# Two batches of an attention layer handled as one unit, with PSUM divided three to five

## Chip, cores, metric

One core of a Trainium2 chip. Times are device microseconds of one execution; the runs of one kernel agree within 0.1% here.

## The reference, cut

Input x is [128 batches, 128 nodes, 512 features], fp32.

```python
# layer 0: h = relu(layernorm(x)); a max over an expression of adj @ h; collapses to one number per node
h = jnp.maximum(_layernorm(x, axis=-1), 0.0)
x = x + _L0_gnn_ref(h, adj, adj, L0_gnn_b)
# layer 1: attention with 8 heads of 64, masked by adj
h = jnp.maximum(_layernorm(x, axis=-1), 0.0)
x = x + _L1_gnn_ref(h, adj, Wq, bq, Wk, bk, Wv, bv)
#   q, k, v = h @ W + b;  scores = q k^T / 8;  masked softmax over j;  out = weights @ v
```

What layer 0 adds is one number per node and batch, and the second layernorm does not see it. So the kernel normalises once, gets layer 0 from one "adjacency" matmul per batch (adj times h, then a maximum), and runs projections, scores and the product with v. A further column of ones in v makes the softmax sums. The projections of four batches are done together, each of q, k and v with seven block products instead of eight (p1 to p7 below; each is a "projection group" of 8 matmuls in the trace). The seven products need sums of blocks of h, which VectorE makes: the "h sums" below.

## The kernel before

```python
        ps_mm = ctx.enter_context(tc.tile_pool(name="ps_mm", bufs=4, space=PSUM))
        ps_sc = ctx.enter_context(tc.tile_pool(name="ps_sc", bufs=1, space=PSUM))
        ps_av = ctx.enter_context(tc.tile_pool(name="ps_av", bufs=1, space=PSUM))
        # ... (cut: loads, constants)
            # norm(m), statistics
            st = stat.tile([P, 6], F32, name="st")
            mv = stat.tile([P, 2], F32, name="mv")
            nc.vector.bn_stats(st, X[g][:, i, :])
            nc.vector.bn_aggr(mv, st)
            ve = stat.tile([P, 1], F32, name="ve")
            nc.vector.tensor_scalar_add(ve, mv[:, 1:2], EPS)
            rstd = RSTD[m] = stat.tile([P, 1], F32, name="rstd")
            nc.gpsimd.tensor_tensor(rstd, ve, mhalf, op=ALU.pow)
            MV[m] = mv

        def norm_end(m):
            g, i = divmod(m, G)
            nc.vector.tensor_scalar(
                HN[m], X[g][:, i, :], MV[m][:, 0:1], 0.0, op0=ALU.subtract, op1=ALU.max
            )
            nc.scalar.activation(HN[m], HN[m], AF.Copy, scale=RSTD[m])
            if m >= G:
                add_bv(m)
        # ... (cut: blocks, move, transposes)
        def adjacency(m):
            g, i = divmod(m, G)
            if m >= 2 * G + 2:
                pa = ps_mm.tile([P, 512], F32, name="mm")
            else:
                if i % 2 == 0:
                    PA[g] = ps_av.tile([P, 2, 512], F32, name="pav")
                pa = PA[g][:, i % 2]
            nc.tensor.matmul(pa, adjT, HN[m], start=True, stop=True)
            nc.vector.reduce_max(AMAX[g][:, i : i + 1], pa, axis=AX.X)
            if i == G - 1:
                nc.vector.tensor_scalar(C[g], AMAX[g], b0_sb, 0.0, op0=ALU.add, op1=ALU.max)
        # ... (cut: the sums of the seven-product scheme, class Products)
            q, k, v = PR[g + 1] = [Products(g + 1, n) for n in "qkv"]
            return (
                (q.p1, last, q.p6, q.p2, q.p7),
                (q.p5, q.p4, k.p1, k.p6, q.p3),
                (k.p2, k.p7, k.p5, k.p4, v.p1),
                (k.p3, v.p6, v.p2, v.p7, v.p5, v.p4),
            )
        # ... (cut)
        def scores(g, i, spare=False):

            psc = ps_sc.tile([P, 2, NC, D], F32, name="sc")
            for f in range(NC):
                for j in range(2):
                    r = slice(j * HD, (j + 1) * HD)
                    nc.tensor.matmul(
                        psc[:, j, f, :],
                        KT[g][r, f, i * D : (i + 1) * D],
                        QT[g][r, f, i * D : (i + 1) * D],
                        start=True, stop=True,
                    )
            if spare:
                w = spare_tile().rearrange("p (j f d) -> p j f d", j=2, f=NC)
            else:
                w = work.tile([P, 2, NC, D], F32, name="w")
            for j in range(2):
                nc.scalar.activation(w[:, j], psc[:, j], AF.Exp, scale=HD ** -0.5)
            return w
        # ... (cut: masks: w *= live, two calls on VectorE)
        def finish(g, i, w, spare=False, eng=nc.vector):
            b = g * G + i
            if spare:
                pav = ps_sc.tile([P, 2, NC, D], F32, name="sc").rearrange("p j f d -> p j (f d)")
            else:
                pav = ps_av.tile([P, 2, 512], F32, name="pav")

            for h in range(H):
                for k in range(2):
                    r = slice(k * HD, (k + 1) * HD)
                    nc.tensor.matmul(
                        pav[r, h // 4, (h % 4) * HE : (h % 4 + 1) * HE],
                        w[:, h % 2, h // 2, r], V[g % 2][:, i, h, :],
                        start=True, stop=True,
                    )
            po = pav[:, :, 0 : 4 * HE].rearrange("p k (h e) -> p k h e", e=HE)
            rs = RS[:, b].rearrange("p (k h) -> p k h", k=2)
            nc.vector.reciprocal(rs, po[:, :, :, HD])
            if b < B - 2:
                o = work.tile([P, 2, 4, HD], F32, name="o")
            else:
                o = tmp.tile([P, 2, HT2], F32, name="p1b").rearrange("p k (h d) -> p k h d", d=HD)
            nc.vector.tensor_tensor(
                o, po[:, :, :, 0:HD], rs.unsqueeze(3).to_broadcast([P, 2, 4, HD]), op=ALU.mult
            )
            y = o.rearrange("p k h d -> p (k h d)")
            x_b, c_b = X[g][:, i, :], C[g][:, i : i + 1]
            if eng is nc.vector:
                eng.scalar_tensor_tensor(y, x_b, c_b, y, op0=ALU.add, op1=ALU.add)
            else:
                nc.scalar.activation(x_b, x_b, AF.Identity, bias=c_b)
                eng.tensor_tensor(y, x_b, y, op=ALU.add)
            nc.sync.dma_start(out[b], y)
        # ... (cut: count, prologue)
            for b in range(B - G - 1):
                g, i = divmod(b, G)
                m = b + 2 * G + 2
                if i == 0 and g + 3 < NG:
                    load(g + 3)
                if i == 0:
                    parts = products(g)
                w = scores(g, i)
                if g == 0:
                    add_bv(b)
                for s in range(max(5, len(parts[i]))):
                    if s < len(parts[i]):
                        parts[i][s]()
                    if s == 0:
                        masks(w)
                    elif s == 3 and b == B - 2 * G + 1:
                        count(0, B - 2 * G)
                    elif i == G - 1 and g + 2 < NG and s < 5:
                        h_sum(g + 2, s - 1)
                    if m < B:
                        if s == 1:
                            norm(m)
                        elif s == 2:
                            norm_end(m)
                        elif s == 4:
                            blocks(m)
                if m < B:
                    adjacency(m)
                finish(g, i, w)
                if m < B:
                    move(m)
            # ... (cut: the last five batches by hand)
```

Of the kernel before, what the change touches and what calls it, by code (L numbers as in the profile page):

```python
# [161 lines left out]
def tile_adj_preln_d2(  # L163
# [36 lines left out]
    def fast(ctx):  # L200
# [5 lines left out]
        ps_mm = ctx.enter_context(tc.tile_pool(name="ps_mm", bufs=4, space=PSUM))  # L206
        ps_sc = ctx.enter_context(tc.tile_pool(name="ps_sc", bufs=1, space=PSUM))
        ps_av = ctx.enter_context(tc.tile_pool(name="ps_av", bufs=1, space=PSUM))

        CNT = []  # L210
        X, HN, TB, HT, HB, QT, KT, C, AMAX, WA, RSTD, MV, PR, PH, PA = ({} for _ in range(15))
# [94 lines left out]
        def transposes(m):  # L306
            g, i = divmod(m, G)
            if i % 2 == 0:
                PH[g] = ps_sc.tile([P, 2, NC, D], F32, name="sc")
            ph = PH[g][:, i % 2]  # L310
            for c in range(NC):
                nc.tensor.transpose(ph[:, c], HN[m][:, c * P : (c + 1) * P], ident)  # L312
            nc.scalar.copy(HT[g][:, i], ph)

        def adjacency(m):
            g, i = divmod(m, G)
            if m >= 2 * G + 2:
                pa = ps_mm.tile([P, 512], F32, name="mm")
            else:
                if i % 2 == 0:  # L320
                    PA[g] = ps_av.tile([P, 2, 512], F32, name="pav")
                pa = PA[g][:, i % 2]
# [149 lines left out]
        def products(g):  # L472


            if g not in PR:
                PR[g] = [Products(g, n) for n in "qkv"]
            last = PR[g][2].p3
            if g + 1 == NG:
                return (last,), (), (), ()
            q, k, v = PR[g + 1] = [Products(g + 1, n) for n in "qkv"]  # L480
            return (
                (q.p1, last, q.p6, q.p2, q.p7),
                (q.p5, q.p4, k.p1, k.p6, q.p3),
                (k.p2, k.p7, k.p5, k.p4, v.p1),
                (k.p3, v.p6, v.p2, v.p7, v.p5, v.p4),
            )
# [6 lines left out]
        def scores(g, i, spare=False):  # L493

            psc = ps_sc.tile([P, 2, NC, D], F32, name="sc")
            for f in range(NC):
                for j in range(2):
                    r = slice(j * HD, (j + 1) * HD)
                    nc.tensor.matmul(  # L499
                        psc[:, j, f, :],  # L500
# [8 lines left out]
            for j in range(2):  # L509
                nc.scalar.activation(w[:, j], psc[:, j], AF.Exp, scale=HD ** -0.5)  # L510
            return w

        def masks(w):
# [3 lines left out]
        def finish(g, i, w, spare=False, eng=nc.vector):  # L517
            b = g * G + i
            if spare:
                pav = ps_sc.tile([P, 2, NC, D], F32, name="sc").rearrange("p j f d -> p j (f d)")  # L520
            else:
                pav = ps_av.tile([P, 2, 512], F32, name="pav")

            for h in range(H):
                for k in range(2):
                    r = slice(k * HD, (k + 1) * HD)
                    nc.tensor.matmul(  # L527
                        pav[r, h // 4, (h % 4) * HE : (h % 4 + 1) * HE],
                        w[:, h % 2, h // 2, r], V[g % 2][:, i, h, :],
                        start=True, stop=True,  # L530
                    )
            po = pav[:, :, 0 : 4 * HE].rearrange("p k (h e) -> p k h e", e=HE)
            rs = RS[:, b].rearrange("p (k h) -> p k h", k=2)
            nc.vector.reciprocal(rs, po[:, :, :, HD])
            if b < B - 2:
                o = work.tile([P, 2, 4, HD], F32, name="o")
            else:
                o = tmp.tile([P, 2, HT2], F32, name="p1b").rearrange("p k (h d) -> p k h d", d=HD)
            nc.vector.tensor_tensor(
                o, po[:, :, :, 0:HD], rs.unsqueeze(3).to_broadcast([P, 2, 4, HD]), op=ALU.mult  # L540
            )
            y = o.rearrange("p k h d -> p (k h d)")
# [19 lines left out]
        with tc.manual_schedule():  # L562
# [43 lines left out]
            move(2 * G + 1)  # L606
            for b in range(B - G - 1):
                g, i = divmod(b, G)
                m = b + 2 * G + 2
                if i == 0 and g + 3 < NG:  # L610
                    load(g + 3)
                if i == 0:
                    parts = products(g)
                w = scores(g, i)
                if g == 0:
                    add_bv(b)
                for s in range(max(5, len(parts[i]))):
                    if s < len(parts[i]):
                        parts[i][s]()
                    if s == 0:  # L620
                        masks(w)
                    elif s == 3 and b == B - 2 * G + 1:
                        count(0, B - 2 * G)
                    elif i == G - 1 and g + 2 < NG and s < 5:
                        h_sum(g + 2, s - 1)
                    if m < B:
                        if s == 1:
                            norm(m)
                        elif s == 2:
                            norm_end(m)  # L630
                        elif s == 4:
                            blocks(m)
                if m < B:
                    adjacency(m)
                finish(g, i, w)
                if m < B:
                    move(m)
# [69 lines left out]
```

## Time and profile before

| | before |
|---|---|
| time, median of 3 runs | 1602.29 us (1601.85 to 1602.46) |
| span of the profiled run | 1599.8 us |
| TensorE busy | 1584.6 us |
| VectorE busy | 1112.2 us (70%) |
| order on TensorE, per batch | adjacency, products with v, scores, 5 or 6 projection groups |

How to read it: what TensorE gets done is read from the starts of its matmuls. A row of the timeline is a run of like instructions: start, length from first start to last end, engine, line, out<-in, the part of the array used (rows*columns), shape, count. The length includes a tail that overlaps the next row (one projection matmul's row is 0.38 us long, the next starts after 0.216); the difference of two starts does not.

### The profile page before, as it was taken

To read this page: it belongs to the slowest core of one execution; us is meant where nothing else is said; L and a number is where in the kernel's file an instruction comes from. 1 tells how busy PE (TensorE), PEld (TensorE's weight loads), DVE (VectorE), ACT (ScalarE), POOL (GpSimd) and SP (SyncE) were. 2 spreads that over 40 slices of the span, in tenths; PEclk is the share of its full clock that TensorE was granted. 3 is DMA by queue.
4 is the path that set the end of the run, shared out by engine and by line. 5 is a ranking of instruction groups with operands and counts; after the bars stand their busy time and mean duration, and the time that the engine had idled before them with its cause. 6 is when DMAs were issued, how large, how long until landed. Compare 5 with 4: busy or idle time off the path is not lost.

```text
span 1599.8 us, 29471 instructions
## 1 busy us (share of the span) xinstructions
PE 1584.6 (99%) x11821; PEld 1319.4 (82%) x11821; DVE 1112.2 (70%) x2044; ACT 424.5 (27%) x848; POOL 264.0 (17%) x281
## 2 busy tenths in 40 slices
PE   7999999999999999999999999999999999999998
PEld 5788888888888888888888888888888888888886
DVE  4777677776777776776767677677777677676655
ACT  3222222222222222222222222222222222222222
POOL 4421111111111111111111111111111111111101
PEclk9999999999999999999999999999999999999999
DMA  4022322123222232222232212322223322223111
GB/s 166 16 69 69 80 64 69 41 70 77 68 65 46 69 73 72 69 48 64 68 80 65 68 42 72 73 68 66 46 69 72 73 69 53 58 68 80 40 28 48
DMA packets 299082, 104.02 MB, mean 65 GB/s; under 512 B 264448, under 2 KB 264576, under 8 KB 298944
## 3 DMA queue, kind: packets, MB, share of 16 engines
q1 hardware_dynamic: 297520, 99.69, 24.8%
q8 instruction: 94, 1.54, 0.4%
q10 hardware_dynamic: 1248, 2.16, 0.4%
q14 instruction: 44, 0.36, 0.1%
q0 software_dynamic: 176, 0.27, 0.1%
HBM read 37.03 MB, written 33.55 MB: 44 GB/s over the span
## 4 chain that ended last, share of the span: by engine, by line
PE 99%; DVE 1%; DMA 0%; ACT 0%; POOL 0%; issue 0%; POOLq 0%; ACTq 0%
PE mm L389 73%; PE sc L499 9%; PE pav L527 8%; PE mm L323 6%; PE mm L460 1%; PE pav L323 1%; PE sc L312 0%; DMA xg<-in_x_dram 0%; DVE tb L515 0%; DVE st L265 0%; DVE amax L324 0%; ACT hn L278 0%; POOL p1b L548 0%; PE sc L527 0%; DVE hn L275 0%
## 5 line engine op out<-in xcount | busy, mean ns | idle before, releaser
L270 POOL TENSOR_TENSOR rstd<-ve,mhalf 128x1 f32<-128x1 f32 x128 | 84.0, 656 | 1210.6 <-DVE ve L268 983.5
L510 ACT ACTIVATE w<-sc 128x512 f32<-128x512 f32 x252 | 136.8, 594 | 505.3 <-PE sc L499 505.3
L527 PEld LDWEIGHTS pav<-v,w 128*64 128x64 f32 x4032 | 127.8, 137 | 91.9 <-issue 47.8
L389 PE MATMUL mm<-hs,sq_sb 128*128 128x256 f32 x744 | 179.0, 383 | 0.0
L389 PE MATMUL mm<-sv_sb,hs 128*128 128x256 f32 x768 | 176.7, 379 | 0.0
L389 PE MATMUL mm<-hs,sk_sb 128*128 128x256 f32 x768 | 176.2, 379 | 0.0
L284 POOL TENSOR_TENSOR xg<-xg,bv_sb 128x512 f32<-128x512 f32 x128 | 163.3, 1277 | 30.2 <-DVE hn L275 28.4
L515 DVE TENSOR_TENSOR w<-w,live 128x512 f32<-128x512 f32 x252 | 162.1, 685 | 2.0 <-ACT w L510 2.0
L389 PEld LDWEIGHTS mm<-hs,sk_sb 128*128 128x128 f32 x768 | 145.9, 190 | 20.7 <-issue 1.0
L389 PEld LDWEIGHTS mm<-sv_sb,hs 128*128 128x128 f32 x768 | 145.8, 190 | 20.4 <-issue 0.5
L278 ACT ACTIVATE hn<-hn,rstd 128x512 f32<-128x512 f32 x126 | 91.4, 725 | 259.7 <-DVE hn L275 207.3
L389 PEld LDWEIGHTS mm<-hs,sq_sb 128*128 128x128 f32 x744 | 138.8, 190 | 21.4
L499 PE MATMUL sc<-qT,kT 64*128 64x128 f32 x2048 | 148.7, 285 | 0.0
L527 PE MATMUL pav<-v,w 128*64 128x65 f32 x4032 | 145.3, 224 | 0.0
L499 PEld LDWEIGHTS sc<-qT,kT 64*128 64x128 f32 x2048 | 124.2, 187 | 10.1 <-issue 1.7
L437 DVE TENSOR_TENSOR u<-mm,p1b 128x512 f32<-128x512 f32 x63 | 43.6, 691 | 126.4 <-PE mm L389 126.4
L389 PE MATMUL mm<-hT,wk_sb 128*128 128x256 f32 x512 | 124.2, 385 | 0.0
L389 PE MATMUL mm<-wv_sb,hT 128*128 128x256 f32 x512 | 121.0, 379 | 0.0
L323 PE MATMUL mm<-hn,adjT 128*128 128x512 f32 x236 | 120.5, 592 | 0.0
L389 PE MATMUL mm<-hT,wq_sb 128*128 128x256 f32 x496 | 120.4, 386 | 0.0
L389 PEld LDWEIGHTS mm<-wv_sb,hT 128*128 128x128 f32 x512 | 97.2, 190 | 13.7 <-issue 0.5
L389 PEld LDWEIGHTS mm<-hT,wk_sb 128*128 128x128 f32 x512 | 94.7, 190 | 15.4
(107 smaller groups left out, 2048.7 us busy)
## 6 DMA issues: line engine op xcount, KB each, us to landing
out_dram<-o SPq DMA_DIRECT2D x126, 256.0 KB, 2.1
xg<-in_x_dram SPq DMA_DIRECT2D x62, 512.0 KB, 5.2
hT<-tb SPq DMA_DIRECT2D x960, 32.0 KB, 1.9
xg<-in_x_dram SPq DMA_DIRECT2D x2, 256.0 KB, 3.3
xg<-in_x_dram ACTq DMA_DIRECT2D x2, 256.0 KB, 6.2
wq_sb<-in_L_gnn_Wq_dram SPq DMA_DIRECT2D x1, 512.0 KB, 8.7
wk_sb<-in_L_gnn_Wk_dram SPq DMA_DIRECT2D x1, 512.0 KB, 11.5
wq_sb<-in_L_gnn_Wq_dram ACTq DMA_DIRECT2D x1, 512.0 KB, 11.4
```

The lines of the kernel that those rows point to most:

```text
L270: nc.gpsimd.tensor_tensor(rstd, ve, mhalf, op=ALU.pow)
L278: nc.scalar.activation(HN[m], HN[m], AF.Copy, scale=RSTD[m])
L284: nc.gpsimd.tensor_tensor(x_m, x_m, bv_sb, op=ALU.add)
L323: nc.tensor.matmul(pa, adjT, HN[m], start=True, stop=True)
L389: nc.tensor.matmul(bank[:, r, :], lhs, rhs, start=first and r == 0 and c == 0, stop=r == 1 and c == 1, skip_group_check=True,)
L437: nc.vector.tensor_tensor(self.u3, self.b, self.pf[1], op=ALU.add)
L460: nc.tensor.matmul(bank[:, r, :], W["q"][:, c, (2 * f + r) * P : (2 * f + r + 1) * P], h[:, :, c], start=r == 0 and c == 0, stop=r == 1 an ...
L499: nc.tensor.matmul(psc[:, j, f, :], KT[g][r, f, i * D : (i + 1) * D], QT[g][r, f, i * D : (i + 1) * D], start=True, stop=True,)
L510: nc.scalar.activation(w[:, j], psc[:, j], AF.Exp, scale=HD ** -0.5)
L515: nc.vector.tensor_tensor(w[:, j], w[:, j], live_h, op=ALU.mult)
L527: nc.tensor.matmul(pav[r, h // 4, (h % 4) * HE : (h % 4 + 1) * HE], w[:, h % 2, h // 2, r], V[g % 2][:, i, h, :], start=True, stop=True,)
```

## The change

Its intent: let TensorE change between its three forms of use (128*128, 128*64, 64*128) once for two batches instead of once for each. For this, products and scores of two batches have to stand side by side, so PSUM, where TensorE's results go, is divided anew. It holds eight banks of 128 x 512 fp32 values in this kernel: before, four for projections, two for scores and two for products; now, three banks for projections, five that the products (banks 0, 1, 2), the scores (3 and 4 for the even batch, 0 and 2 for the odd one), the adjacency products (0, 1) and the first transposes share. Heads 0 to 6 of a batch fill one bank, head 7 of both goes into bank 1. The loop is rewritten in units of two batches.

```diff
-        ps_mm = ctx.enter_context(tc.tile_pool(name="ps_mm", bufs=4, space=PSUM))
-        ps_sc = ctx.enter_context(tc.tile_pool(name="ps_sc", bufs=1, space=PSUM))
-        ps_av = ctx.enter_context(tc.tile_pool(name="ps_av", bufs=1, space=PSUM))
+        ps_mm = ctx.enter_context(tc.tile_pool(name="ps_mm", bufs=3, space=PSUM))
+        ps_at = ctx.enter_context(tc.tile_pool(name="ps_at", bufs=1, space=PSUM))
...  (adjacency: pa = bank(i % 2); scores: banks (3, 4) or (0, 2))
-                (q.p1, last, q.p6, q.p2, q.p7),
-                (q.p5, q.p4, k.p1, k.p6, q.p3),
-                (k.p2, k.p7, k.p5, k.p4, v.p1),
-                (k.p3, v.p6, v.p2, v.p7, v.p5, v.p4),
+                (q.p1, last, q.p6, q.p2, q.p7, q.p5, q.p4, k.p1, q.p3, k.p6),
+                (k.p2, k.p7, k.p5, k.p4, v.p1, k.p3, v.p6, v.p2, v.p7, v.p5, v.p4),
...  (finish is split: apply(b) has the products of two batches and their evictions, residual(b) the rest)
+        def apply(b):
+            one = bank(0), bank(1), bank(2)
+            for e in range(2):
+                g, i = divmod(b + e, G)
+                w = w_of.pop(b + e)
+                for h in range(H):
+                    pav, c = (one[2 * e], h * HE) if h < H - 1 else (one[1], e * HE)
...  (two matmuls each; then reciprocal and multiplication for bank 0, bank 2, bank 1)
+            for b in range(0, B - 3 * G // 2, 2):
...
+                if b > 0:
+                    apply(b - 2)
+                scores(b)
+                scores(b + 1)
+                for s, p in enumerate(part):
+                    if s < 2:
+                        if b > 0:
+                            residual(b - 2 + s)
+                        masks(b + s)
+                    p()
...
+                    if m < B:
+                        if s in (2, 4):
+                            norm(m + s // 2 - 1)
+                        elif s in (3, 5):
+                            norm_end(m + s // 2 - 1)
+                        elif s in (6, 7):
+                            blocks(m + s - 6)
+                        if s in (4, 7):
+                            adjacency(m + s // 7)
+                    if i == 2 and g + 2 < NG and 7 <= s < 11:
+                        h_sum(g + 2, s - 7)
...  (the last six batches are rewritten by hand)
```

More of the change, by code (lines that the diff above doesn't have):

```diff
@@ L205, in fast, with bank @@
         stat = ctx.enter_context(tc.tile_pool(name="stat", bufs=6))
-        ps_mm = ctx.enter_context(tc.tile_pool(name="ps_mm", bufs=4, space=PSUM))
-        ps_sc = ctx.enter_context(tc.tile_pool(name="ps_sc", bufs=1, space=PSUM))
-        ps_av = ctx.enter_context(tc.tile_pool(name="ps_av", bufs=1, space=PSUM))
-        CNT = []
-        X, HN, TB, HT, HB, QT, KT, C, AMAX, WA, RSTD, MV, PR, PH, PA = ({} for _ in range(15))
+        ps_mm = ctx.enter_context(tc.tile_pool(name="ps_mm", bufs=3, space=PSUM))
+        ps_at = ctx.enter_context(tc.tile_pool(name="ps_at", bufs=1, space=PSUM))
+        CNT, w_of, O = [], {}, {}
+        X, HN, TB, HT, HB, QT, KT, C, AMAX, WA, RSTD, MV, PR = ({} for _ in range(13))
+        def bank(k):
+            return ps_at.tile([P, 512], F32, name=f"at{k}")
         def load(g):
@@ L307, in transposes @@
             g, i = divmod(m, G)
-            if i % 2 == 0:
-                PH[g] = ps_sc.tile([P, 2, NC, D], F32, name="sc")
-            ph = PH[g][:, i % 2]
+            ph = bank(3 + i % 2).rearrange("p (c d) -> p c d", c=NC)
             for c in range(NC):
@@ L316, in adjacency @@
             g, i = divmod(m, G)
-            if m >= 2 * G + 2:
-                pa = ps_mm.tile([P, 512], F32, name="mm")
-            else:
-                if i % 2 == 0:
-                    PA[g] = ps_av.tile([P, 2, 512], F32, name="pav")
-                pa = PA[g][:, i % 2]
+            pa = bank(i % 2)
             nc.tensor.matmul(pa, adjT, HN[m], start=True, stop=True)
@@ L472, in products @@
         def products(g):
-            if g not in PR:
-                PR[g] = [Products(g, n) for n in "qkv"]
             last = PR[g][2].p3
             if g + 1 == NG:
-                return (last,), (), (), ()
+                return (last,), ()
             q, k, v = PR[g + 1] = [Products(g + 1, n) for n in "qkv"]
             return (
-                (q.p1, last, q.p6, q.p2, q.p7),
-                (q.p5, q.p4, k.p1, k.p6, q.p3),
-                (k.p2, k.p7, k.p5, k.p4, v.p1),
-                (k.p3, v.p6, v.p2, v.p7, v.p5, v.p4),
+                (q.p1, last, q.p6, q.p2, q.p7, q.p5, q.p4, k.p1, q.p3, k.p6),
+                (k.p2, k.p7, k.p5, k.p4, v.p1, k.p3, v.p6, v.p2, v.p7, v.p5, v.p4),
             )
@@ L491, in spare_tile, with scores @@
             return t.rearrange("p a i c r -> p (a i c r)")
-        def scores(g, i, spare=False):
-            psc = ps_sc.tile([P, 2, NC, D], F32, name="sc")
+        def scores(b, spare=False):
+            g, i = divmod(b, G)
+            psc = [
+                bank(k).rearrange("p (f d) -> p f d", f=NC) for k in ((3, 4), (0, 2))[b % 2]
+            ]
             for f in range(NC):
@@ L499, in scores @@
                     nc.tensor.matmul(
-                        psc[:, j, f, :],
+                        psc[j][:, f, :],
                         KT[g][r, f, i * D : (i + 1) * D],
@@ L509, in scores, with masks @@
             for j in range(2):
-                nc.scalar.activation(w[:, j], psc[:, j], AF.Exp, scale=HD ** -0.5)
-            return w
-        def masks(w):
+                nc.scalar.activation(w[:, j], psc[j], AF.Exp, scale=HD ** -0.5)
+            w_of[b] = w
+        def masks(b):
+            w = w_of[b]
             for j in range(2):
                 nc.vector.tensor_tensor(w[:, j], w[:, j], live_h, op=ALU.mult)
-        def finish(g, i, w, spare=False, eng=nc.vector):
-            b = g * G + i
-            if spare:
-                pav = ps_sc.tile([P, 2, NC, D], F32, name="sc").rearrange("p j f d -> p j (f d)")
-            else:
-                pav = ps_av.tile([P, 2, 512], F32, name="pav")
-            for h in range(H):
-                for k in range(2):
-                    r = slice(k * HD, (k + 1) * HD)
-                    nc.tensor.matmul(
-                        pav[r, h // 4, (h % 4) * HE : (h % 4 + 1) * HE],
-                        w[:, h % 2, h // 2, r], V[g % 2][:, i, h, :],
-                        start=True, stop=True,
-                    )
-            po = pav[:, :, 0 : 4 * HE].rearrange("p k (h e) -> p k h e", e=HE)
-            rs = RS[:, b].rearrange("p (k h) -> p k h", k=2)
-            nc.vector.reciprocal(rs, po[:, :, :, HD])
-            if b < B - 2:
-                o = work.tile([P, 2, 4, HD], F32, name="o")
-            else:
-                o = tmp.tile([P, 2, HT2], F32, name="p1b").rearrange("p k (h d) -> p k h d", d=HD)
-            nc.vector.tensor_tensor(
-                o, po[:, :, :, 0:HD], rs.unsqueeze(3).to_broadcast([P, 2, 4, HD]), op=ALU.mult
-            )
-            y = o.rearrange("p k h d -> p (k h d)")
@@ new lines, in apply @@
+        def apply(b):
[5 more added lines that the diff above has]
+                    pav, c = (one[2 * e], h * HE) if h < H - 1 else (one[1], e * HE)
+                    for k in range(2):
+                        r = slice(k * HD, (k + 1) * HD)
+                        nc.tensor.matmul(
+                            pav[r, c : c + HE], w[:, h % 2, h // 2, r], V[g % 2][:, i, h, :],
+                            start=True, stop=True,
+                        )
+            if b < B - 2:
+                o = work.tile([P, 2, N], F32, name="o", bufs=1)
+            else:
+                o = proj.tile([P, 4, 2, 2, D], F32, name="hs").rearrange(
+                    "p k i c d -> p k (i c d)"
+                )[:, 0:2]
+            O[b] = o
+            for e, h, n in ((0, 0, 7), (1, 0, 7), (None, 7, 1)):
+                if e is None:
+                    po = one[1][:, 0 : 2 * HE].rearrange("p (e h) -> p e h", h=HE)
+                    rs = RS[:, b : b + 2, 7]
+                    oo = o[:, :, 7 * HD : N]
+                else:
+                    po = one[2 * e][:, 0 : 7 * HE].rearrange("p (h e) -> p h e", e=HE)
+                    rs = RS[:, b + e, 0:7]
+                    oo = o[:, e, 0 : 7 * HD].rearrange("p (h d) -> p h d", d=HD)
+                nc.vector.reciprocal(rs, po[:, :, HD])
+                nc.vector.tensor_tensor(
+                    oo, po[:, :, 0:HD],
+                    rs.unsqueeze(2).to_broadcast([P, rs.shape[1], HD]), op=ALU.mult,
+                )
@@ L543, in finish, with residual @@
+        def residual(b, eng=nc.vector):
+            g, i = divmod(b, G)
+            y = O[b - b % 2][:, b % 2]
             x_b, c_b = X[g][:, i, :], C[g][:, i : i + 1]
@@ L605, in fast @@
                     h_sum(1, s - 8)
-            move(2 * G + 1)
-            for b in range(B - G - 1):
+            for b in range(0, B - 3 * G // 2, 2):
                 g, i = divmod(b, G)
-                m = b + 2 * G + 2
-                if i == 0 and g + 3 < NG:
-                    load(g + 3)
                 if i == 0:
                     parts = products(g)
-                w = scores(g, i)
-                if g == 0:
-                    add_bv(b)
-                for s in range(max(5, len(parts[i]))):
-                    if s < len(parts[i]):
-                        parts[i][s]()
-                    if s == 0:
-                        masks(w)
-                    elif s == 3 and b == B - 2 * G + 1:
-                        count(0, B - 2 * G)
-                    elif i == G - 1 and g + 2 < NG and s < 5:
-                        h_sum(g + 2, s - 1)
-                    if m < B:
-                        if s == 1:
-                            norm(m)
-                        elif s == 2:
-                            norm_end(m)
-                        elif s == 4:
-                            blocks(m)
-                if m < B:
-                    adjacency(m)
-                finish(g, i, w)
-                if m < B:
-                    move(m)
@@ L640, in fast @@
-            g = NG - 1
-            k3, v6, v2, v7, v5, v4 = parts[G - 1]
-            w = scores(g - 1, G - 1)
-            k3()
-            masks(w)
+                part = parts[i // 2]
+                m = b + 2 * G + 2
+                if b > 0:
[8 more added lines that the diff above has]
+                    p()
+                    if s == 1 and i == 0:
+                        if g + 3 < NG:
+                            load(g + 3)
+                        if m <= B:
+                            move(m - 1)
+                    if s == 8 and i == 0 and m < B:
+                        move(m + 1)
+                    if s == 1 and g == 0:
+                        add_bv(b)
+                        add_bv(b + 1)
+                    if m < B:
+                        if s in (2, 4):
[8 more added lines that the diff above has]
+                        h_sum(g + 2, s - 7)
+                    if b == B - 2 * G and s == 7:
+                        count(0, b)
@@ L645, in fast @@
+            k2, k7, k5, k4, v1, k3, v6, v2, v7, v5, v4 = parts[1]
+            b = B - 6
+            apply(b - 2)
+            scores(b)
+            scores(b + 1)
+            for s, p in enumerate((k2, k7, k5, k4, k3)):
+                p()
+                if s < 2:
+                    residual(b - 2 + s)
+                    masks(b + s)
+            apply(b)
+            scores(b + 2)
+            scores(b + 3)
+            v1()
+            residual(b)
+            residual(b + 1)
             v6()
-            w0 = scores(g, 0)
+            masks(b + 2)
@@ L647, in fast @@
             v2()
-            masks(w0)
-            finish(g - 1, G - 1, w)
+            masks(b + 3)
+            scores(b + 4, spare=True)
             v7()
-            w1 = scores(g, 1)
+            scores(b + 5, spare=True)
             v5()
-            masks(w1)
-            w2 = scores(g, 2, spare=True)
-            v4()
-            masks(w2)
-            w3 = scores(g, 3, spare=True)
-            finish(g, 0, w0, eng=nc.gpsimd)
-            masks(w3)
-            PR[g][2].p3()
-            finish(g, 1, w1, eng=nc.gpsimd)
@@ L662, in fast @@
-            finish(g, 2, w2, spare=True, eng=nc.gpsimd)
-            finish(g, 3, w3)
+            masks(b + 4)
+            v4()
+            masks(b + 5)
+            apply(b + 2)
+            PR[NG - 1][2].p3()
+            apply(b + 4)
+            for k in range(4):
+                residual(b + 2 + k, nc.vector if k == 3 else nc.gpsimd)
             count(B - 2 * G, B)
```

## The prediction

> **What bounds the kernel now.** I read the page first, then TensorE's waits, then the timeline of one batch in the steady part.
>
> ```profile
> PE 1584.6 (99%) x11821; PEld 1319.4 (82%) x11821; DVE 1112.2 (70%) x2044; ACT 424.5 (27%) x848; POOL 264.0 (17%) x281
> ...
> PE 99%; DVE 1%; DMA 0%; ACT 0%; POOL 0%; issue 0%; POOLq 0%; ACTq 0%
> ```
>
> TensorE is busy for the whole span and is 99% of the chain that ended last; VectorE at 70% is the next engine. TensorE's waits add up to some 12 us, all in the first 17 and last 10 us. So the time is the sum of TensorE's stream, and the change can only gain by shortening that stream. A busy share of 99% hides what lies between matmuls, so I read starts, not durations (timeline of TensorE, one batch: start, length, line, count).
>
> ```profile
> 600.78 1.02 PE L323 MATMUL mm<-hn,adjT 128*128 128x512 f32 x2
> 601.73 1.15 PE L527 MATMUL pav<-v,w 128*64 128x65 f32 x32
> 602.82 1.16 PE L499 MATMUL sc<-qT,kT 64*128 64x128 f32 x16
> 603.91 1.99 PE L389 MATMUL mm<-hT,wq_sb 128*128 128x256 f32 x8
> 605.74 1.89 PE L389 MATMUL mm<-sv_sb,hT 128*128 128x256 f32 x8
> 607.46 1.89 PE L389 MATMUL mm<-hs,sq_sb 128*128 128x256 f32 x8
> 609.19 1.89 PE L389 MATMUL mm<-hT,wq_sb 128*128 128x256 f32 x8
> 610.92 1.89 PE L389 MATMUL mm<-hs,sq_sb 128*128 128x256 f32 x8
> ```
>
> Projection groups follow each other at 1.727 us (605.74, 607.46, 609.19, 610.92), 0.216 us a matmul. The column before the shape is what matters: the array is used as 128*128, then 128*64 (products with v), then 64*128 (scores), then 128*128 again. Three changes of form per batch, each with a price:
> - adjacency to product: 601.73 - 600.78 = 0.95 us for two 128x512 matmuls that need 2 x 0.429 = 0.858 (two of 256 columns need 0.432). Excess 0.09.
> - products: 1.09 us to the first score. Their own rate comes from two windows that begin inside the group:
>
> ```profile
> 602.01 0.87 PE L527 MATMUL pav<-v,w 128*64 128x65 f32 x24
> ...
> 602.60 0.29 PE L527 MATMUL pav<-v,w 128*64 128x65 f32 x4
> ```
>
> 20 matmuls, that is 10 pairs running side by side, in 0.59 us: 0.059 a pair, 16 pairs 0.944. Excess 0.14.
> - scores: 603.91 - 602.82 = 1.09 us. Windows read in the same way give 0.112 a pair, so 8 pairs are 0.896. Excess 0.195.
> - the first projection group after the scores takes 605.74 - 603.91 = 1.83 against 1.727. Excess 0.105.
>
> Sum: 0.53 us per batch, 0.18 per change of form. Over some 125 batches that is 66 us of 1602 in which TensorE counts as busy and does little.
>
> **What the Trainium skill says.** "TensorEngine Tiling (Array Packing)", Overview, Tiling Modes, Key Properties: "Changing tiling mode (not just tile) drains the TensorE". The trace agrees, with 0.18 us a change. "Perfetto Trace Analysis", Tensor Engine Instruction: the end of a matmul in a profile is computed from its size, not observed; this fits a drain that shows as no idle time at all. "PSUM — Partial Sum Buffer", summary rules: guard PSUM with semaphores by bank. Here it means that a score may overwrite a bank of the products only when VectorE has read all of it; no wait of that kind is in the trace before, since both had banks of their own.
>
> **The change, part by part.**
>
> 1. *Changes of form removed.* After it, two batches share one triple (products of two, scores of two). Before: 122 full triples in the loop and about 17 changes around it, 383 in all. After: 60 triples and about 15, 195 in all. 188 changes x 0.18 = 33 us gained. Matmul work is the same.
>
> 2. *Banks of projections, four to three.* Of q, k and v each keeps three accumulators. In the new order a bank is taken again only after at least two other groups (3.4 us) since its last reading began, but for those whose reader is one group back: the v bank read by the last addition has the products, the scores and two groups between. VectorE reads 0.2 us after a group ends, for 0.69. No wait: 0.
>
> 3. *Scores of the odd batch now go into banks 0 and 2, which the products have just filled.* Count from the first product, T = 0. Bank 0 is full at about 0.81 (14 pairs at 0.059), VectorE can start 0.26 later (602.67 to 602.93 in the trace), 1.07; bank 2 is full at 1.75, readable at 2.01. Reciprocal 0.21 plus hand-over 0.04, multiplication 0.63 (0.69 for 512 columns, here 448): bank 2 is free at 2.01 + 0.25 + 0.63 = 2.89. TensorE wants it at 2.02 (products) + 1.00 (even scores) = 3.02. It just fits. Where VectorE still has the last v addition and one h sum to do (every second pair), it comes free at 0.11 + 0.61 + 0.61 = 1.33 and bank 2 at about 3.0 to 3.1. Wait 0 to 0.1 us, x 30: 1.5 us lost.
>
> 4. *The adjacency product comes too early for its input.* Before, the normalisation ended (line 275, 278) after the third group of a batch and the adjacency product came at least two groups later. Now, for the even batch of a pair, it ends at step 3 and the product stands right after step 4: one group. What the chain needs, in the timeline before, is here (group starts 609.19 and 610.92 above):
>
> ```profile
> 609.28 0.15 DVE L268 TENSOR_SCALAR ve<-mv 128x1 f32<-128x1 f32 x1
> 609.46 0.69 DVE L428 TENSOR_TENSOR u<-mm,p1a 128x512 f32<-128x512 f32 x1
> 609.58 0.55 POOL L270 TENSOR_TENSOR rstd<-ve,mhalf 128x1 f32<-128x1 f32 x1 [10.71 <-DVE ve L268]
> 610.07 0.48 DVE L275 TENSOR_SCALAR hn<-xg,mv 128x512 f32<-128x512 f32 x1
> 610.66 0.72 ACT L278 ACTIVATE hn<-hn,rstd 128x512 f32<-128x512 f32 x1 [3.16 <-DVE hn L275]
> ```
>
> VectorE adds the group's result first (609.46), then line 275 (610.07), then ScalarE scales (610.66 to 611.38): 2.19 us after the group ended at 609.19; another batch, without an overlap of 0.07, shows 2.12. One group is 1.73. So with steps 2 and 3 both ending in a VectorE addition (k.p5, k.p4: the second pair of each four) TensorE waits 2.16 + 0.04 - 1.73 = 0.47 us. In the first pair step 3 is q.p2, which ScalarE evicts: line 275 runs at once, ScalarE is done with two evictions at +1.02, GpSimd's rstd comes at about +1.0, the scaling ends at +1.75: wait 0.06. The odd batch has two groups between and waits for nothing. 29 x 0.47 + 30 x 0.06 = 15.4 us lost.
>
> 5. *VectorE:* three reciprocals and multiplications for two batches instead of two of each; 0.3 to 0.5 us more per pair of 24 us, beside TensorE. 0.
>
> 6. *Ends.* At the start transposes and adjacency get a bank each instead of half of a shared double bank: perhaps 0.7 us gained. At the end the last products, of two batches, need the last v addition right before them (about 1 us wait, where the kernel before waited 1.0 us too), then three multiplications, and GpSimd's last addition may hold VectorE's up. I put 1 us lost. Sum -0.3.
>
> Sum: 33 - 1.5 - 15.4 - 0.3 = 16 us gained. **1586 us.**
>
> **Rivals.**
> - *A: the drains go and nothing takes their place.* 1602 - 33 = 1569, just over 2% faster. For it: the drain is regular in every batch and needs no assumption. Against: the chain of step 4 is 0.4 us longer than one group in the trace before, and there is no other work of TensorE to put there.
> - *B: VectorE becomes the bound around the pair.* After the products it has three evictions, two residuals (0.75 each) and four masks (0.65 each), some 6 us in one piece; if it falls behind, the scores and the projection banks wait. Against: by my count it is through with the masks of the odd batch at T + 7.3, just before the first addition is ready at T + 7.8. If it were 0.3 us late in each pair, 60 x 0.3 = 18 us, the gain is gone: 1604.
> - *C: three banks stall the projections.* A reader late by over 1 us would be needed. If it cost 0.2 us a pair: 1598.
> - *D: two batches in one form change rate.* If the longer product and score groups ran slower, by bank alternation, each per cent of 4 us is 0.04 us a pair, 2.5 us in all. Nothing speaks for it.
>
> **Range and chances.** The 33 us are sure within 2. The waits of step 4 are the soft part: from 8 (if the chain is 0.2 us shorter) to 22 (if the first pair waits as well as the second); the scores' wait goes from 0 to 6. Low end 33 - 6 = 27 gained: 1575 and a little below; high end 33 - 22 - 6 - 3 = 2 gained: 1599. Range 1572 to 1599. Two per cent is 1570, which needs rival A almost pure: 0.13. Slower by 2% needs B in force: 0.04.
>
> **What would show each step right or wrong.** Step 1: in the timeline a pair of batches shows one change to 128*64 and one to 64*128, products of two taking 2.02 us and scores 1.99 to the next group. Step 3: TensorE's waits list the second scores' line on VectorE's multiplication, under 3 us in total. Step 4: they list the adjacency line on ScalarE's scaling, about 15 us in all, with a longest near 0.5, in every second pair. Steps 2 and B are wrong if projections wait on VectorE or ScalarE by more than a few us. The prediction fails if the adjacency waits are missing (then 1570), or if the waits of the scores are of the size of half a microsecond per pair (then 1600 and more).

## The result

The changed kernel took 1600.10 us (median of 4 runs, 1599.99 to 1600.49), the kernel before in the same rounds 1602.07. The ratio is 0.9988, 95% interval 0.9971 to 1.0006. Predicted were 1586 us and a range of 1572 to 1599: of 16 us, 2 came.

The page of the changed kernel, first the engines, then the chain that ended last:

```profile
PE 1572.3 (98%) x11821; PEld 1316.8 (82%) x11821; DVE 1113.5 (70%) x2172; ACT 421.2 (26%) x848; POOL 253.9 (16%) x281
...
PE 91%; DVE 6%; ACT 2%; issue 1%; DMA 0%; POOL 0%; ACTq 0%; DVEq 0%; SPq 0%; POOLq 0%
```

The matmuls are the same in number (11821). TensorE's share of the chain falls from 99 to 91%, and VectorE and ScalarE have come into it: TensorE now waits for VectorE's and ScalarE's results inside the loop. The view of TensorE's waits says for what (us in total, times, longest):

```profile
PE at L320 <- ACT hn L282: 9.5, 32, 0.6
```

Line 320 is the adjacency product, line 282 ScalarE's scaling. The timeline of TensorE over two pairs of batches shows this and more:

```profile
598.96 2.09 PE L526 MATMUL at<-v,w 128*64 128x65 f32 x64
600.98 2.20 PE L495 MATMUL at<-qT,kT 64*128 64x128 f32 x32
603.11 1.99 PE L386 MATMUL mm<-hT,wq_sb 128*128 128x256 f32 x8
...
610.12 1.89 PE L386 MATMUL mm<-hs,sq_sb 128*128 128x256 f32 x8
612.04 1.12 PE L320 MATMUL at<-hn,adjT 128*128 128x512 f32 x2
613.00 1.89 PE L386 MATMUL mm<-hs,sq_sb 128*128 128x256 f32 x8
...
618.18 1.02 PE L320 MATMUL at<-hn,adjT 128*128 128x512 f32 x2
619.04 1.89 PE L386 MATMUL mm<-hT,sq_sb 128*128 128x256 f32 x8
...
624.60 2.14 PE L495 MATMUL at<-qT,kT 64*128 64x128 f32 x32
626.67 1.99 PE L386 MATMUL mm<-hT,wk_sb 128*128 128x256 f32 x8
...
633.68 1.89 PE L386 MATMUL mm<-wv_sb,hT 128*128 128x256 f32 x8
635.86 1.13 PE L320 MATMUL at<-hn,adjT 128*128 128x512 f32 x2 [0.28 <-ACT hn L282]
636.82 1.89 PE L386 MATMUL mm<-hT,sk_sb 128*128 128x256 f32 x8
```

The first pair shown runs q's projection groups; VectorE still has an h sum to do when its products begin. The second runs k's and v's and has no h sum there. Below they are the first and the second kind of pair. Read the rows by differences of starts:
- The products of two batches take 600.98 - 598.96 = 2.02 us, as predicted: one change of form for two batches.
- The even batch's adjacency product starts 612.04 - 610.12 = 1.92 us after the group before it, which needs 1.73: 0.19 late. In the second pair it is 2.18: 0.45 late.
- Once started, the two adjacency matmuls of these places take 0.96 us (613.00 - 612.04 and 636.82 - 635.86). The odd batch's, which waits for nothing, takes 0.86 (618.18 to 619.04). So each wait costs 0.10 more after it has ended.
- The scores of two batches take 2.13 us to the next group in the first pair and 2.07 in the second, where 16 pairs of 0.112 and one change make 1.99. No wait is listed for this.

Summed in this way over the 59 pairs that have an adjacency product, from the starts in the trace: late start 19.7 us, longer first matmul 6.1 us; and over the 63 pairs of scores 6.9 us. That is 32.7 us, nearly all of the 33 that the changes of form had cost. The list of waits shows 9.5 of it, and the row at 612.04 has none listed: a projection matmul's row is 0.38 us long though the next could start after 0.216, so the first 0.16 us of a wait count as busy, and the 0.03 left of 0.19 are too short for the list.

### The profile page after: what moved, and what is told of

Same layout as the page of the kernel before. It is cut to its first block, busy times and chain, and to the rows that moved or that the text cites. A ratio compares the mean times of both kernels' runs of the same rounds, so it can differ in the third digit from the quotient of the medians.

```text
span 1597.9 us, 29802 instructions
## 1 busy us (share of the span) xinstructions
PE 1572.3 (98%) x11821; PEld 1316.8 (82%) x11821; DVE 1113.5 (70%) x2172; ACT 421.2 (26%) x848; POOL 253.9 (16%) x281
## 4 chain that ended last, share of the span: by engine, by line
PE 91%; DVE 6%; ACT 2%; issue 1%; DMA 0%; POOL 0%; ACTq 0%; DVEq 0%; SPq 0%; POOLq 0%
PE mm L386 66%; PE at L495 8%; PE at L526 8%; PE at L320 8%; DVE kT L407 2%; ACT hn L282 2%; DVE st L269 1%; PE mm L457 1%; DVE hn L279 1%; DVE mv L270 0%; PE at L314 0%; DVE ve L272 0%; DMA hT<-tb 0%; DMA xg<-in_x_dram 0%; DVE v L407 0%
## 5 line engine op out<-in xcount | busy, mean ns | idle before, releaser
L274 POOL TENSOR_TENSOR rstd<-ve,mhalf 128x1 f32<-128x1 f32 x128 | 75.0, 586 | 1097.5 <-DVE ve L272 707.3
L506 ACT ACTIVATE w<-at 128x512 f32<-128x512 f32 x252 | 130.1, 602 | 450.6 <-PE at L495 450.6
L386 PE MATMUL mm<-hs,sq_sb 128*128 128x256 f32 x744 | 175.6, 379 | 0.0
L320 PE MATMUL at<-hn,adjT 128*128 128x512 f32 x252 | 136.3, 623 | 10.3 <-ACT hn L282 9.5
L321 DVE TENSOR_REDUCE amax<-at 128x1 f32<-128x512 f32 x128 | 88.1, 688 | 83.4 <-PE at L320 83.4
L526 PEld LDWEIGHTS at<-v,w 128*64 128x64 f32 x4032 | 122.9, 137 | 21.3 <-issue 20.9
L495 PE MATMUL at<-qT,kT 64*128 64x128 f32 x2048 | 138.7, 281 | 0.0
L526 PE MATMUL at<-v,w 128*64 128x65 f32 x4032 | 131.7, 223 | 0.2 <-DVE v L407 0.2
L425 DVE TENSOR_TENSOR u<-mm,p1a 128x512 f32<-128x512 f32 x95 | 65.7, 692 | 95.0 <-PE mm L386 94.4
L495 PEld LDWEIGHTS at<-qT,kT 64*128 64x128 f32 x2048 | 126.2, 187 | 5.3 <-issue 1.0
```

The source lines that it names most:

```text
L386: nc.tensor.matmul(bank[:, r, :], lhs, rhs, start=first and r == 0 and c == 0, stop=r == 1 and c == 1, skip_group_check=True,)
L425: nc.vector.tensor_tensor(self.u2, self.b, self.pf[0], op=ALU.add)
L495: nc.tensor.matmul(psc[j][:, f, :], KT[g][r, f, i * D : (i + 1) * D], QT[g][r, f, i * D : (i + 1) * D], start=True, stop=True,)
L506: nc.scalar.activation(w[:, j], psc[j], AF.Exp, scale=HD ** -0.5)
L526: nc.tensor.matmul(pav[r, c : c + HE], w[:, h % 2, h // 2, r], V[g % 2][:, i, h, :], start=True, stop=True,)
```

## The experiments

All but the last are edits of the changed kernel, and all gave correct results. The theory: the gain is there in full, and is given back in the three terms above. The rivals: VectorE is the real bound and what is taken away will come back elsewhere; three banks are too few; the changes of form never cost what the gaps said.

### The adjacency product one group later

```diff
-                        if s in (4, 7):
+                        if s in (5, 7):
                             adjacency(m + s // 7)
```

> One change to the changed kernel: the even batch's adjacency product stands one projection group later, two groups after its normalisation instead of one. Theory (the product waits for ScalarE's scaling, and each wait also leaves one weight load uncovered): of the 25.8 us that these 59 places cost in the changed kernel (19.7 us late start, 6.1 us longer first matmul) all come back: 1574 us, TensorE's list of waits without the adjacency line, the two adjacency matmuls 0.43 us apart everywhere. Rival (VectorE is the real bound and the wait only moves to the scores or to a projection): over 1590 us, with new waits on VectorE. Rival (only the listed wait of 9.5 us is lost time): 1590 us.

Measured: 1574.25 us (1574.01 to 1574.44), ratio to the kernel before 0.9826 (0.981 to 0.9843); 25.8 us less than the changed kernel's median. In TensorE's waits the line shrinks to one case, in the start:

```profile
PE at L320 <- ACT hn L282: 0.2, 1, 0.2
```

and in the timeline the even batch's product takes 0.86 us, like the odd batch's (a pair of the first kind; the second kind is the same):

```profile
604.00 1.02 PE L320 MATMUL at<-hn,adjT 128*128 128x512 f32 x2
604.86 1.89 PE L386 MATMUL mm<-hs,wq_sb 128*128 128x256 f32 x8
```

The whole of late start and longer first matmul came back, not the 9.5 us of the list. VectorE is not the bound: nothing else began to wait.

### The normalisation one step earlier instead

```diff
-                        if s in (2, 4):
-                            norm(m + s // 2 - 1)
-                        elif s in (3, 5):
-                            norm_end(m + s // 2 - 1)
+                        if s in (1, 4):
+                            norm(m + s // 4)
+                        elif s in (2, 5):
+                            norm_end(m + s // 4)
```

> The adjacency product stays where the changed kernel has it, but the even batch's normalisation starts one step earlier, so that its chain (VectorE, GpSimd, ScalarE) has one group more. Theory: the place in TensorE's order is harmless, only the chain's lateness counts: the same 1574 us as with the later product, within 3. Rival (the place between these two projection groups is itself costly): 1600 us, first adjacency matmul still 0.53 us. Second rival (the earlier normalisation delays VectorE's additions after the masks, so projections wait): between 1580 and 1600 with waits of projections on VectorE.

Measured: 1574.12 us, a single run (state unknown; it agrees with the run before within 0.2 us). Its list of waits has the same single case of 0.2 us for the line. The place of the product in TensorE's order is harmless. What counted was the distance to the chain that feeds it.

### Head 7 of both batches last

```diff
-            for e in range(2):
+            ws = [w_of.pop(b + e) for e in range(2)]
+            for e, heads in ((0, range(H - 1)), (1, range(H - 1)), (0, (H - 1,)), (1, (H - 1,))):
                 g, i = divmod(b + e, G)
-                w = w_of.pop(b + e)
-                for h in range(H):
+                w = ws[e]
+                for h in heads:
```

> One change to the changed kernel: the products of head 7 of both batches come last, so bank 2 is full 0.12 us earlier. Theory (the odd batch's second half of scores starts late because VectorE frees bank 2 less than one weight load ahead): in the pairs where VectorE was free the lag of 0.08 us goes; in the pairs where VectorE still has an addition and an h sum to do (lag 0.14) it stays. 29 x 0.08 = 2.3 us less: 1598 us. Rival (the lag comes from the change of bank or row tile within the scores, not from VectorE): 1600 us, both lags unchanged.

Measured: 1597.69 us (1597.34 to 1597.88), ratio 0.9973; 2.4 us less than the changed kernel. The timeline, one pair of each kind:

```profile
600.11 2.20 PE L495 MATMUL at<-qT,kT 64*128 64x128 f32 x32
602.24 1.99 PE L386 MATMUL mm<-hT,wq_sb 128*128 128x256 f32 x8
...
623.74 2.06 PE L495 MATMUL at<-qT,kT 64*128 64x128 f32 x32
625.72 1.99 PE L386 MATMUL mm<-hT,wk_sb 128*128 128x256 f32 x8
```

The second kind fell from 2.07 to 1.98 us, the first kept its 2.13: as the theory has it, and against the rival that the change of bank itself costs.

### The h sums one step earlier as well

```diff
-                    if i == 2 and g + 2 < NG and 7 <= s < 11:
-                        h_sum(g + 2, s - 7)
+                    if i == 2 and g + 2 < NG and 6 <= s < 10:
+                        h_sum(g + 2, s - 6)
```

> As the run before, and the four h sums one step earlier, so VectorE is free when bank 0 is full in every pair. Theory: both lags go, the products' and scores' groups of a pair take 2.02 and 1.99 us everywhere: 6.7 us less than the changed kernel, 1593 us. Rival (not VectorE): 1600 us.

Measured: 1593.23 us (1592.91 to 1593.89), ratio 0.9946; 6.9 us less than the changed kernel. Both kinds of pair now take 1.98 us for the scores. VectorE's evictions of a pair of the first kind show why. First the changed kernel, whose products began at 598.96:

```profile
599.68 0.68 DVE L338 TENSOR_TENSOR hs<-hT,hs 128x512 f32<-128x512 f32 x1
600.28 0.20 DVE L546 RECIPROCAL RS<-at 128x7 f32<-128x7 f32 x1
600.51 0.62 DVE L547 TENSOR_TENSOR o<-at,RS 128x448 f32<-128x448 f32 x1
601.05 0.19 DVE L546 RECIPROCAL RS<-at 128x7 f32<-128x7 f32 x1
601.28 0.62 DVE L547 TENSOR_TENSOR o<-at,RS 128x448 f32<-128x448 f32 x1
```

Then this run, whose products began at 596.80:

```profile
597.88 0.21 DVE L547 RECIPROCAL RS<-at 128x7 f32<-128x7 f32 x1 [0.28 <-PE at L527]
598.12 0.62 DVE L548 TENSOR_TENSOR o<-at,RS 128x448 f32<-128x448 f32 x1
598.70 0.21 DVE L547 RECIPROCAL RS<-at 128x7 f32<-128x7 f32 x1
598.94 0.62 DVE L548 TENSOR_TENSOR o<-at,RS 128x448 f32<-128x448 f32 x1
```

Bank 2 is free at 601.90, 2.94 us after the products' start, in the changed kernel, and at 599.56, 2.76 us after it, here. The odd scores are due at 3.02, yet 2.94 was too late, by 0.14. In the changed kernel's second kind VectorE was done with bank 2 at 625.46, 2.87 after 622.59, and that was still late by 0.08.

### All three edits together

> The later adjacency product together with head 7 last and the earlier h sums. Theory: the three repaired terms add up, since all lie in TensorE's own stream: 1600.1 - 25.8 - 6.9 = 1567.4 us, 2.2% faster than the kernel before; TensorE waits for nothing between the first 20 and the last 12 us, and a pair of batches takes the sum of its matmuls plus one triple of changes. Rival (with TensorE 2% faster VectorE cannot follow and new waits take part of it back): 1570 to 1575 us.

Measured: 1567.93 us (1567.54 to 1568.61), the kernel before 1602.22 in the same rounds, ratio 0.9789, interval 0.9772 to 0.9805. It is the fastest kernel of this study and beats both; whether it is more than 2% faster than the kernel before the interval leaves open. The terms add up to within 0.5 us (1567.4 expected). The page's chain, and one pair in the timeline:

```profile
PE 97%; DMA 1%; DVE 1%; issue 0%; POOL 0%; ACT 0%; ACTq 0%; POOLq 0%; DVEq 0%
```

```profile
610.54 2.09 PE L527 MATMUL at<-v,w 128*64 128x65 f32 x64
612.55 2.06 PE L495 MATMUL at<-qT,kT 64*128 64x128 f32 x32
614.54 1.99 PE L386 MATMUL mm<-hT,wk_sb 128*128 128x256 f32 x8
```

2.01 us of products, 1.99 of scores, and no wait of TensorE in the loop.

### The scores of a pair torn apart again

The run before with one edit: `scores(b + 1)` is moved from directly after `scores(b)` to behind the pair's first projection group (`if s == 0: scores(b + 1)` after `p()`).

> As the run before, but one projection group stands between the scores of the two batches of a pair: the same matmuls, with two changes of form more per pair and nothing else that could wait. Theory (a change of form costs what the gaps in the kernel before said, 0.20 + 0.19 us for leaving and entering the scores): 61 x 0.39 = 24 us more than the run before, 1591 us, with no wait in TensorE's list. Rival (the drain is only an accounting effect of pipelined starts, and the gain of the change came from elsewhere): under 1572 us.

Measured: 1591.90 us (1591.62 to 1592.00), ratio 0.9937; 24.0 us more than the run before, for the 61 pairs of the loop: 0.39 us for two changes of form. TensorE's list has no wait in the loop. One pair in the timeline:

```profile
621.76 1.16 PE L495 MATMUL at<-qT,kT 64*128 64x128 f32 x16
622.86 1.99 PE L386 MATMUL mm<-hT,wk_sb 128*128 128x256 f32 x8
624.78 1.16 PE L495 MATMUL at<-qT,kT 64*128 64x128 f32 x16
625.87 3.72 PE L386 MATMUL mm<-hs,sk_sb 128*128 128x256 f32 x16
629.43 0.81 PE L386 MATMUL mm<-hs,wk_sb 128*128 128x256 f32 x3
```

The scores take 1.10 and 1.09 us, 0.20 more than the 1.99 of both at once; the group between them takes 1.92 where the first group after the scores has 1.83 in the run before (614.54 to 616.37 there), and the two after it 3.56 where two among others take 3.45. Together 0.40 us. This is the cost that the change set out to remove, measured by itself for entering and for leaving the scores; the change from adjacency to products was not tested alone.

### The kernel before with three banks for the projections

```diff
-        ps_mm = ctx.enter_context(tc.tile_pool(name="ps_mm", bufs=4, space=PSUM))
+        ps_mm = ctx.enter_context(tc.tile_pool(name="ps_mm", bufs=3, space=PSUM))
+        ps_ad = ctx.enter_context(tc.tile_pool(name="ps_ad", bufs=1, space=PSUM))
...
-                pa = ps_mm.tile([P, 512], F32, name="mm")
+                pa = ps_ad.tile([P, 512], F32, name="pad")
```

> The kernel before with only one part of the change: three banks for the projections and one of its own for the adjacency product, scores and products as they were. Theory: three banks are enough, no waits, 1602 us within 0.2%. Rival (the fourth bank absorbed VectorE's late additions, so the change lost time by the division too): 1606 us or more, with waits of projections on VectorE.

Measured: 1601.65 us (1601.42 to 1602.22), ratio 0.9999 (0.9982 to 1.0015). The division of PSUM costs nothing measurable here. In the old order, that is: in the new one it is the runs above that show no wait of a projection.

## Why the prediction was wrong

Two steps failed, 4 and 3. Both expected the right wait in the right place, but priced it by the lateness against the matmul's start alone; the traces show these waits at the weight load before it. Step 4 also had one producer's chain too short.

*The bound, and step 1 (33 us gained from 188 changes of form): right.* The kernel with all three repairs is 34.3 us below the kernel before, and the torn pairs put the price of a change into or out of the scores at 24.0 / 122 = 0.197 us. (The traces count 384 and 196 changes; 33 is 188 x 0.53 / 3, while 188 x 0.18 would be 34.) With the losses measured the prediction's own sum is 33 - 25.8 - 6.9 - 0.3 = 0; the 2 us that remained are not assigned.

*Steps 2 and 5 (banks of the projections, VectorE's additional evictions: 0): right*, by the three-bank run and by TensorE's lists of waits. VectorE's reciprocals and multiplications grew by 19.7 us in all, 0.31 for each of 64 pairs, off TensorE's path but for step 3. *Step 6 (ends, -0.3): not tested by itself;* the 34.3 against 33 leaves it within about a microsecond.

*Step 4 (the adjacency product comes too early, 15.4 us lost): the mechanism right, the size wrong; 25.8 us.* The sum is 19.7 of lateness, where 15.4 was all that was counted, and 6.1 of longer first matmuls. Two terms of its sum failed.
- The second kind's 0.47 us was 0.45. But the step took a wait to cost its lateness only. After each wait the first adjacency matmul takes 0.10 us more, 59 times. The view of weight loads (PEld) shows what differs. In the kernel before, the adjacency matmul starts at 612.64 and its weights are loaded a matmul ahead:

```profile
612.43 0.41 PEld L323 LDWEIGHTS mm<-hn,adjT 128*128 128x128 f32 x2
```

In the changed kernel the wait holds the weight load, though its weights (adjT) never change; load and matmul both start at 612.04:

```profile
612.04 0.30 PEld L320 LDWEIGHTS at<-hn,adjT 128*128 128x128 f32 x2 [0.43 <-ACT hn L282]
```

  "TensorE: Matmul & The Clock Gate", Step-by-step and LDWEIGHTS, says that the engine can pull weight loads ahead of running matmuls, and gives columns divided by 1.2 in ns for one load: an estimate of 107 ns for 128 columns. In this trace a load's row is 0.19 us long, but the two loads of the row above take 0.30 together, so the second begins 0.11 us after the first. The 0.10 us fit one uncovered load. That it is this load is read from the trace; no run here separates it from other costs of a restart. The trace's records also say where the wait stands: in the operands of the first weight load of 123 of the 128 adjacency products (127 in the kernel before), and of none of their matmuls. So it is the compiled program that puts this wait on the load; what a wait on the matmul alone would cost, no run shows.
- The first kind's 0.06 us was 0.19, which makes most of the 4.3 us of lateness above the 15.4 (30 x 0.13 = 3.9). The step had GpSimd's rstd ready 1.0 us after the group; it came at 1.12:

```profile
610.28 0.15 DVE L272 TENSOR_SCALAR ve<-mv 128x1 f32<-128x1 f32 x1
610.58 0.66 POOL L274 TENSOR_TENSOR rstd<-ve,mhalf 128x1 f32<-128x1 f32 x1 [18.56 <-DMA hT<-tb]
...
611.27 0.72 ACT L282 ACTIVATE hn<-hn,rstd 128x512 f32<-128x512 f32 x1
```

  610.12 is the end of the group of step 3. Line 272, which rstd needs, starts 0.07 us later after it than in the rows that I had used (610.28 after 610.12 against 609.28 after 609.19), and rstd takes 0.66 instead of 0.55 us; the scaling, waiting for it, ends at 611.99. The 0.55 was the short kind of a time that varies: rstd's 128 cases in the kernel before have a mean of 0.66. ScalarE's start at 611.27 fits an end at 611.24. The step's sum had no margin for any of this.

*Step 3 (the odd scores in banks 0 and 2, "it just fits", 1.5 us lost): 6.9 us.* The times at which the banks come free were right, or even too late (2.87 in the trace, 2.89 in the text; 2.94 against "3.0 to 3.1"). What failed is the time at which they are wanted: I took the start of the first score, 3.02, but the wait sits at its weight load, which would start 0.11 us earlier, and freeing has to reach it. The trace has that load at 602.02 in the first kind and at 625.58 in the second, each 0.12 us after the multiplication's end (601.90, 625.46): the step had no hand-over back to TensorE. So bank 2 has to be free by 3.02 - 0.11 - 0.12 = 2.79. At 2.94 that is 0.15 late (0.14 lost), at 2.87 it is 0.08 (0.08 lost), and at 2.76 nothing was lost.

*The signs.* The prediction looked for its losses in the list of waits: about 15 us for step 4, under 3 for step 3. The list has 9.5 and nothing, so of the 32.7 us it hides 23; the differences of starts show them.

*Rivals.* A was not far from what the kernel could do once repaired (1569 against 1568), but not as changed. B and C fell with the first and the last experiment. D did not occur: products of two batches take the 2.02 us, and repaired scores the 1.99, that the old rates give. The stated range allowed the waits of step 4 22 us and of step 3 6 at most; both went beyond at once, and the result lies 1 us outside. The range's own sums slip too: 2 us gained is 1600, not 1599, and its low end takes 6 us off where step 4's least wait is 8.

## What to carry to other kernels

Here each wait on TensorE cost its lateness plus 0.10 us, most likely the weight load that could no longer run ahead. So count a matmul's due time from its weight load, with the hand-over before it (0.11 + 0.12 us for the scores here); one step more of distance cost nothing in these runs. Merging phases to save changes of form shortens the steps that other chains had been hiding behind: list each producer's latency against its new distance, and give margins under 0.2 us the price of a miss. In a kernel at 99% TensorE, sum the differences of starts, not the idle time.

## What the Trainium skill lacked or had wrong

- "TensorEngine Tiling (Array Packing)", Key Properties, says that a change of tiling mode drains the engine, but gives no price. Here (fp32) leaving or entering the scores cost 0.197 us (24.0 us for 122 changes), and a triple of changes 0.53: about 0.09 us before each first matmul and 0.05 (64 columns) to 0.10 us (128 columns) in it, by the starts in the kernel before. The second part again looks like an uncovered weight load; no run shows that it is one.
- "Perfetto Trace Analysis", Tensor Engine Instruction, says that a matmul's end is computed, but not what follows for reading waits: 25.8 us lost at 59 waits stood as 9.5 us of idle time.
- No page says that a wait for the moving operand can be put on the weight load, as in this program, and what a held load costs; here 0.10 us more per wait (59 of them, 6.1 us), with constant weights.
- For scores on two row tiles side by side: one of two tiles held up 0.08 to 0.14 us by its bank does not catch up while the group lasts (2.07 and 2.13 us instead of 1.99; in the group of 600.98 it is 0.15 us behind the other tile at its second score and at its last). No page has it.
